# Rows of a graph attention kernel: TensorE turns replaced by a DRAM scratch and a broadcasting transfer

## Chip, cores, metric

One core of one Trainium2 chip. The metric is the device time of one execution in microseconds (us), lower is better.

## What is computed

Sixteen graphs of 1024 nodes with 256 features pass through four graph attention layers. Each layer is of this form (the four differ in the leaky function and in what follows):

```python
h  = relu(layernorm(x))
Wh = h @ W
f1, f2 = Wh @ a[:F], Wh @ a[F:]
e  = leaky_relu(f1[:, :, None] + f2[:, None, :])
e  = where(adj == 0, -1e9, e)
x  = x + softmax(e, -1) @ Wh          # layer 3: four heads of 64, then a normalisation
```

The exponential of a leaky sum is the larger (or smaller) of two products of exponentials. So the kernel needs no exponential for an edge: the weight of an edge is `max(r[i], c[j])`, times the mask, where r is a row vector and c a column. VectorE makes it with one instruction for 128 x 512 edges; such an instruction is called a weighing here. A turn is a transposition on TensorE: it takes a column of numbers, one in each of the 128 partitions, and lays it out as a row. SBUF is the memory that the engines work from, PSUM the one that TensorE writes to.

## The kernel before, where the change and the argument touch it

Two streams of batches (even and odd) are generators. Each `yield t` adds t to the stream's clock, and the stream that is behind goes on; this ranks their work. The built order interleaves them more finely than the text does. Each engine runs its own instructions in that order.

```python
    def weigh(column, c, mask, op, half, into):
        turned = psum.tile([P, HALF], F32, name="misc", bufs=3)
        for n in range(NG):                               # NG = 4 turns for a half row
            nc.tensor.transpose(
                turned[:, ts(n, P)], column(half * NG + n).to_broadcast([P, P]), ident)
        r = rows.tile([P, HALF], F32, name="row")
        nc.scalar.copy(r, turned)
        w = edges.tile([P, NI, HALF], F32, name="weights")
        into.append(w)
        for j in range(NI):                               # 8 weighings on VectorE
            nc.vector.scalar_tensor_tensor(
                w[:, j, :], r, c(j), mask[:, j, ts(half, HALF)], op0=op, op1=ALU.mult)
            if j % 4 == 3:
                yield 1.5

    # attend(), layers 0 to 2: first half's weights, then eight row blocks
            yield from weighing[0]
            for i in range(NI):
                t = next(weighing[1], None)
                ...
                for j in range(NI):
                    nc.tensor.matmul(acc, w[:, j, ts(i % NG, P)], V[:, j, : D + 1], ...)
                finish(i, acc)
                yield 3.6
                if i % 2 == 0 and i > 0:
                    project(then, xb, i // 2 - 1, following[1])   # the next layer's V, two blocks
                    yield 4.0

    # layer 3, for each of 4 heads x 2 halves
            for j in range(NI):
                nc.tensor.matmul(accT, V3[:, j, h, :], w[:, j, :], ...)
            sums = wide.tile([E + 1, HALF], F32, name="sums")
            nc.scalar.copy(sums, accT)
            next(coming, None)          # a step of the load of a later batch
            yield 7.5
            acc = psum.tile([P, NG, E + 1], F32, name="misc", bufs=3)
            for i in range(NG):
                nc.tensor.transpose(acc[:, i, :], sums[:, ts(i, P)], ident[: E + 1, : E + 1])
            ...
            yield 0.5

    streams = [[0.0, stream(0)], [LAG, stream(1)]]      # LAG = 120.0
```

Column `D + 2` of V (in layer 3, the last third of `ex`) gives a row.

## Time and profile before

| | before |
|---|---|
| time, median of 3 | 3343.65 us (3341.39 to 3344.26) |
| TensorE / VectorE / ScalarE busy | 93 / 75 / 29% |
| mean granted TensorE clock | 0.988 |

PE is TensorE and PEld its weight loads, DVE is VectorE, ACT ScalarE, POOL GpSimd, SP the engine that issues transfers. A busy share alone does not tell the bound; the prediction shows the lines that do.

### The profile page before, as it was taken

To read this page: it belongs to the slowest core of one execution; us is meant where nothing else is said; L and a number is where in the kernel's file an instruction comes from. 1 tells how busy PE (TensorE), PEld (TensorE's weight loads), DVE (VectorE), ACT (ScalarE), POOL (GpSimd) and SP (SyncE) were. 2 spreads that over 40 slices of the span, in tenths; PEclk is the share of its full clock that TensorE was granted. 3 is DMA by queue.
4 is the path that set the end of the run, shared out by engine and by line. 5 is a ranking of instruction groups with operands and counts; after the bars stand their busy time and mean duration, and the time that the engine had idled before them with its cause. 6 is when DMAs were issued, how large, how long until landed. Compare 5 with 4: busy or idle time off the path is not lost.

```text
span 3341.3 us, 38569 instructions
## 1 busy us (share of the span) xinstructions
PE 3103.0 (93%) x13702; PEld 2107.8 (63%) x13702; DVE 2504.0 (75%) x6140; ACT 974.3 (29%) x2081; POOL 1091.2 (33%) x1286
## 2 busy tenths in 40 slices
PE   6899999999989999899998999989999899998987
PEld 5765756657656675665756667566666666656652
DVE  5677787777778777787777877778777787777766
ACT  3423323232232322323233232332323223232121
POOL 1223324233242332424234142242323423234242
PEclk9999999999999999999999999999999999999998
DMA  4101101011010110101011010010101101000000
GB/s 115 26 4 16 32 11 40 7 17 29 13 39 8 16 29 13 38 10 16 26 16 35 10 42 4 13 35 13 39 4 17 32 13 38 7 10 13 1 13 14
DMA packets 55192, 73.19 MB, mean 22 GB/s; under 512 B 4049, under 2 KB 37969, under 8 KB 54993
## 3 DMA queue, kind: packets, MB, share of 16 engines
q0 software_dynamic: 18432, 33.56, 6.7%
q1 hardware_dynamic: 36560, 37.10, 3.5%
q8 instruction: 110, 1.80, 0.2%
q14 instruction: 90, 0.73, 0.1%
HBM read 87.43 MB, written 16.78 MB: 31 GB/s over the span
## 4 chain that ended last, share of the span: by engine, by line
DVE 45%; PE 42%; POOL 5%; ACT 4%; issue 3%; DMA 1%; SPq 0%; ACTq 0%; POOLq 0%; DVEq 0%
DVE weights L255 25%; PE acc L338 18%; PE acc L414 11%; PE projected L236 10%; DVE above L226 3%; PE misc L230 3%; DVE above L273 2%; DVE stats L220 2%; DVE above L274 2%; POOL x_b L275 2%; DVE V L290 2%; DVE y L380 1%; POOL y L379 1%; POOL rstd L212 1%; ACT below L271 1%
## 5 line engine op out<-in xcount | busy, mean ns | idle before, releaser
L338 PE MATMUL acc<-V,weights 128*128 128x257 f32 x6144 | 1454.9, 385 | 12.5 <-DVE weights L255 11.5
L338 PEld LDWEIGHTS acc<-V,weights 128*128 128x128 f32 x6144 | 1137.8, 191 | 208.9 <-DVE weights L255 47.2
L414 PE MATMUL acc<-weights,V 128*65 128x512 f32 x2048 | 914.2, 593 | 0.3 <-DVE weights L255 0.3
L255 DVE SCALAR_TENSOR_TENSOR weights<-row,ex,mask 128x512 f32<-128x512 f32 x1024 | 762.7, 784 | 2.7 <-ACT row L251 0.9
L255 DVE SCALAR_TENSOR_TENSOR weights<-row,V,mask 128x512 f32<-128x512 f32 x768 | 559.4, 776 | 53.0 <-ACT row L251 52.9
L414 PEld LDWEIGHTS acc<-weights,V 128*65 128x65 f32 x2048 | 278.7, 138 | 492.7 <-issue 474.0
L212 POOL TENSOR_TENSOR rstd<-rstd,minus_half 128x2 f32<-128x2 f32 (+1 forms) x320 | 311.3, 975 | 745.7 <-DVE rstd L211 703.2
L236 PE MATMUL projected<-W,hT 128*128 128x259 f32 (+1 forms) x2048 | 521.8, 398 | 14.8 <-ACT hT L232 11.3
L236 PEld LDWEIGHTS projected<-W,hT 128*128 128x128 f32 x2048 | 383.5, 195 | 130.1 <-ACT hT L232 60.4
L275 POOL TENSOR_TENSOR x_b<-x_b,above 128x256 f32<-128x256 f32 x256 | 227.5, 890 | 585.8 <-DVE above L274 532.5
L230 PE MATMUL misc<-ident,above 128*128 128x128 f32 x1024 | 189.1, 289 | 155.3 <-DVE above L226 108.6
L271 ACT ACTIVATE below<-acc,inv 128x256 f32<-128x256 f32 x256 | 120.0, 472 | 607.4 <-DVE inv L264 497.0
L232 ACT COPY hT<-misc 128x512 f32<-128x512 f32 x256 | 149.1, 586 | 495.8 <-PE misc L230 494.8
L230 PEld LDWEIGHTS misc<-ident,above 128*128 128x128 f32 x1024 | 113.7, 143 | 256.0 <-DVE above L226 120.3
L220 DVE BATCH_NORM_STATS2 stats<-x_b 128x6 f32<-128x256 f32 x512 | 206.7, 414 | 83.1 <-POOL x_b L275 78.9
L263 DVE TENSOR_SCALAR inv<-acc 128x1 f32<-128x1 f32 x256 | 37.3, 150 | 272.5 <-PE acc L338 272.3
L418 ACT COPY sums<-acc 65x512 f32<-65x512 f32 x128 | 74.0, 578 | 546.2 <-PE acc L414 546.1
L226 DVE TENSOR_SCALAR above<-x_b,mv 128x256 f32<-128x256 f32 x512 | 222.0, 443 | 3.8 <-POOL x_b L275 1.7
L105 POOL DMA_DIRECT2D adj_i<-in_adj_dram x128 | 77.1, 603 | 406.3 <-ACT sums L418 174.4
L290 DVE TENSOR_SCALAR V<-projected,rstd,V 128x256 f32<-128x256 f32 x256 | 134.8, 537 | 63.9 <-ACT V L286 62.9
L286 ACT ACTIVATE V<-projected,rstd 128x3 f32<-128x3 f32 x384 | 99.4, 261 | 262.0 <-PE projected L236 220.1
L314 POOL TENSOR_TENSOR x_b<-x_b,beta 128x256 f32<-128x256 f32 x128 | 117.3, 923 | 150.7 <-DVE above L226 148.6
(70 smaller groups left out, 2370.1 us busy)
## 6 DMA issues: line engine op xcount, KB each, us to landing
adj_i<-in_adj_dram POOLq DMA_DIRECT2D x128, 256.0 KB, 3.8
x_b<-in_x_dram SPq DMA_DIRECT2D x16, 1024.0 KB, 7.8
out_dram<-y SPq DMA_DIRECT2D x32, 512.0 KB, 3.8
W<-in_L_gnn_W_dram SPq DMA_DIRECT2D x3, 256.0 KB, 3.0
a_b<-in_L_gnn_a_dram SPq DMA_DIRECT2D x3, 256.0 KB, 6.4
a_b<-in_L_gnn_a_src_dram SPq DMA_DIRECT2D x1, 640.0 KB, 7.5
a_b<-in_L_gnn_a_dst_dram SPq DMA_DIRECT2D x1, 640.0 KB, 9.4
W<-in_L_gnn_W_dram SPq DMA_DIRECT2D x2, 128.0 KB, 8.9
```

The costliest lines, as they stand in the source:

```text
L212: nc.gpsimd.tensor_tensor(r, r, minus_half.to_broadcast([P, n]), op=ALU.pow)
L220: nc.vector.bn_stats(stats, xb[:, 2 * pair + n, :])
L226: nc.vector.tensor_scalar(above, xb[:, 2 * pair + n, :], mv[:, n, 0:1], 0.0, op0=ALU.subtract, op1=ALU.max)
L230: nc.tensor.transpose(turned[:, k, ts(n, P)], above[:, ts(k, P)], ident)
L232: nc.scalar.copy(hT, turned)
L236: nc.tensor.matmul(projected, hT[:, k, ts(n, P)], W[l][:, k, :], start=(k == 0), stop=(k == NK - 1),)
L255: nc.vector.scalar_tensor_tensor(w[:, j, :], r, c(j), mask[:, j, ts(half, HALF)], op0=op, op1=ALU.mult)
L271: nc.scalar.activation(below, acc[:, :D], AF.Exp, scale=inv)
L275: nc.gpsimd.tensor_add(xi, xi, above)
L290: nc.vector.tensor_scalar(V[:, i, :D], projected[:, :D], rstd, V[:, i, D : D + 1], op0=ALU.mult, op1=ALU.mult,)
L338: nc.tensor.matmul(acc, w[:, j, ts(i % NG, P)], V[:, j, : D + 1], start=(j == 0), stop=(j == NI - 1),)
L414: nc.tensor.matmul(accT, V3[:, j, h, :], w[:, j, :], start=(j == 0), stop=(j == NI - 1))
```

## The change

The intent: take 896 turns of 128x128 off the busiest engine and 224 row copies off ScalarE. The eight columns of a row are turned once, as a block of 8 x 128 (32 x 128 for layer 3's four heads), copied, written to DRAM in a line of 1024 numbers, and read back by one transfer that gives the line to all 128 partitions. To find room in SBUF, buffers are cut, and in layer 3 the four turns of the sums follow their matmuls at once.

```diff
+    def lay(b, columns, n):
+        turned = psum.tile([P, HALF], F32, name="misc", bufs=3)[: n * NI, :P]
+        nc.tensor.transpose(turned, columns, ident)
+        flat = wide.tile([P, P], F32, name="flat", bufs=1)[: n * NI]
+        nc.scalar.copy(flat, turned)
+        laid = dram.tile([n, N], F32, name=f"laid{b % 2}_{n}")
+        nc.sync.dma_start(laid.rearrange("n (i p) -> (n i) p", p=P), flat)
+        return laid
+
+    def spread(b, laid):
+        r = rows.tile([P, N], F32, name=f"row{b % 2}")
+        nc.sync.dma_start(r, on_all_partitions(laid, N))
+        return r
 # attend()
+            r = spread(b, lay(b, V[:, :, D + 2], 1)[0])
+            yield 0.5
 # layer 3
+        laid = lay(b, ex[:, 2 * H :, :].rearrange("p h i -> p (h i)"), H)
+        spreads = [spread(b, laid[h]) for h in range(2)]
         def weigh3(n):
+                if half == 0 and 0 < h < H - 1:
+                    spreads.append(spread(b, laid[h + 1]))
-            sums = wide.tile([E + 1, HALF], F32, name="sums")
+            sums = wide.tile([P, HALF], F32, name="wide")[: E + 1]
             nc.scalar.copy(sums, accT)
-            next(coming, None)
-            yield 7.5
             ...                                # turns of the sums, division
-            yield 0.5
+            next(coming, None)
+            yield 8.0
 # cut: the turns in weigh; rows bufs 4 -> 2 (of twice the size), below bufs 3 -> 2, ones moved,
 # ex stored heads first
```

More of the change, by code (lines that the diff above doesn't have):

```diff
@@ L85, in short_path @@
     nc.vector.memset(minus_half, -0.5)
-    ones = const.tile([P, P], F32, name="ones")
-    nc.vector.memset(ones, 1.0)
     squares = const.tile([P, B, NI], F32, name="squares")
@@ L146, in short_path @@
     with tc.tile_pool(name="prep", bufs=2) as prep:
+        ones = prep.tile([P, P], F32, name="ones")
+        nc.vector.memset(ones, 1.0)
         for l in range(3):
@@ L200, in short_path @@
     edges = ctx.enter_context(tc.tile_pool(name="edges", bufs=4))
-    rows = ctx.enter_context(tc.tile_pool(name="rows", bufs=4))
+    rows = ctx.enter_context(tc.tile_pool(name="rows", bufs=2))
+    dram = ctx.enter_context(tc.tile_pool(name="dram", bufs=2, space=bass.MemoryType.DRAM))
     single = ctx.enter_context(tc.tile_pool(name="single", bufs=1))
@@ L240, in project, with lay, spread, weigh @@
             evict(2 * pair + n, projected, rstd[:, n : n + 1])
-    def weigh(column, c, mask: bass.AP, op, half: int, into: list):
-        turned = psum.tile([P, HALF], F32, name="misc", bufs=3)
-        for n in range(NG):
-            nc.tensor.transpose(
-                turned[:, ts(n, P)], column(half * NG + n).to_broadcast([P, P]), ident
-            )
-        r = rows.tile([P, HALF], F32, name="row")
-        nc.scalar.copy(r, turned)
+    def lay(b: int, columns: bass.AP, n: int) -> bass.AP:
+        turned = psum.tile([P, HALF], F32, name="misc", bufs=3)[: n * NI, :P]
[5 more added lines that the diff above has]
+        return laid
+    def spread(b: int, laid: bass.AP) -> bass.AP:
+        r = rows.tile([P, N], F32, name=f"row{b % 2}")
+        nc.sync.dma_start(r, on_all_partitions(laid, N))
+        return r
+    def weigh(r: bass.AP, c, mask: bass.AP, op, half: int, into: list):
         w = edges.tile([P, NI, HALF], F32, name="weights")
@@ L255, in weigh @@
             nc.vector.scalar_tensor_tensor(
-                w[:, j, :], r, c(j), mask[:, j, ts(half, HALF)], op0=op, op1=ALU.mult
+                w[:, j, :], r[:, ts(half, HALF)], c(j), mask[:, j, ts(half, HALF)], op0=op, op1=ALU.mult
             )
@@ L269, in add_elu @@
         inverse(inv, acc[:, D : D + 1])
-        below = work.tile([P, D], F32, name="below")
+        below = work.tile([P, D], F32, name="below", bufs=2)
         nc.scalar.activation(below, acc[:, :D], AF.Exp, scale=inv)
@@ L302, in begin3 @@
             V3 = nodes.tile([P, NI, H, E + 1], F32, name="V")
-            ex = last["ex"] = small.tile([P, NI, 3 * H], F32, name="ex", bufs=2)
+            ex = last["ex"] = small.tile([P, 3 * H, NI], F32, name="ex", bufs=2)
             def evict3(i: int, projected: bass.AP, rstd: bass.AP):
-                nc.scalar.activation(ex[:, i, :], projected[:, D:], AF.Exp, scale=rstd)
+                nc.scalar.activation(ex[:, :, i], projected[:, D:], AF.Exp, scale=rstd)
                 nc.scalar.mul(h3[:, i, :], projected[:, :D], rstd)
-                q = ex[:, i, :H].unsqueeze(2)
+                q = ex[:, :H, i : i + 1]
                 nc.gpsimd.tensor_mul(
@@ L321, in attend @@
             halves = []
+            r = spread(b, lay(b, V[:, :, D + 2], 1)[0])
+            yield 0.5
             weighing = [
-                weigh(
-                    lambda i: V[:, i, D + 2 : D + 3], lambda j: V[:, j, D + 1 : D + 2],
-                    mask, op, half, halves,
-                )
+                weigh(r, lambda j: V[:, j, D + 1 : D + 2], mask, op, half, halves)
                 for half in range(NH)
@@ L400, in weigh3 @@
             if h < H:
+                if half == 0 and 0 < h < H - 1:
+                    spreads.append(spread(b, laid[h + 1]))
                 yield from weigh(
-                    lambda i: ex[:, i, 2 * H + h : 2 * H + h + 1],
-                    lambda j: ex[:, j, H + h : H + h + 1], mask, ALU.max, half, halves,
+                    spreads[h], lambda j: ex[:, H + h, j : j + 1], mask, ALU.max, half, halves
                 )
```

## The prediction

> **What bounds the kernel now.** I read first the page's busy table, to see which engine has least room.
>
> ```profile
> span 3341.3 us, 38569 instructions
> PE 3103.0 (93%) x13702; PEld 2107.8 (63%) x13702; DVE 2504.0 (75%) x6140; ACT 974.3 (29%) x2081; POOL 1091.2 (33%) x1286
> ```
>
> TensorE (PE) is busy 93% of the span, VectorE (DVE) 75%, ScalarE (ACT) 29%. Next the chain that ended last, since a share of busy time does not say who makes whom wait:
>
> ```profile
> DVE 45%; PE 42%; POOL 5%; ACT 4%; issue 3%; DMA 1%; SPq 0%; ACTq 0%; POOLq 0%; DVEq 0%
> ```
>
> The end is reached through TensorE and VectorE by turns. So TensorE time taken out is worth nearly its full size only where TensorE is the one that is behind; elsewhere VectorE's weights (25% of the chain, line 255) decide. Third, the groups by line, for the instructions that the change removes:
>
> ```profile
> L247 PE MATMUL misc<-ident,ex 128*128 128x128 f32 x512 | 77.6, 272 | 0.0
> L247 PE MATMUL misc<-ident,V 128*128 128x128 f32 x384 | 63.6, 276 | 2.3 <-ACT mask L122 1.8 <-ACT V L286 0.3
> L251 ACT COPY row<-misc 128x512 f32<-128x512 f32 x224 | 129.5, 587 | 89.4 <-PE misc L247 88.6
> L255 DVE SCALAR_TENSOR_TENSOR weights<-row,V,mask 128x512 f32<-128x512 f32 x768 | 559.4, 776 | 53.0 <-ACT row L251 52.9
> ```
>
> 896 turns (512 in layer 3, 384 in layers 0 to 2) are busy 141.2 us, but busy time of pipelined matmuls contains their tails. What a turn costs TensorE is the distance between starts, and the chain in order of time, between 1636 and 1665 us, shows that where TensorE is the one that is behind:
>
> ```profile
> 1642.80 0.66 PE misc L247 x6
> 1643.46 3.47 PE acc L338 x16
> 1646.93 6.87 PE acc L414 x16
> ```
>
> Six turns in 0.66 us: 0.11 us each, against 0.27 us in the group's mean. Likewise 0.217 us for a layer 0-2 attention matmul and 0.429 us for a layer 3 one. Last I looked at the stretches of the span. Two stages alternate: stretches with a layer 3 in one of the two batch streams, and stretches with attention of layers 0 to 2 in both.
>
> ```profile
> 960.00:1020.00 60.00, 51.28 (x242) 39.95 (x241) 45.18 (x125) 17.85 (x42) 32.18 (x43) 0.97 0.17 44
> 1020.00:1160.00 140.00, 135.78 (x596) 86.82 (x595) 104.99 (x251) 42.25 (x86) 39.27 (x42) 1.00 0.09 14
> ```
>
> The columns after the length are busy time of TensorE, its weight loads, VectorE, ScalarE and GpSimd. TensorE is 97% busy in the second kind (a layer 3), only 85% in the first, where two streams wait on their own chains (normalise, turn, project, weigh).
>
> **What the Trainium skill says.** (1) "Perfetto Trace Analysis", Identifying the Most-Contended Engine: matmul busy time is no good measure, since pipelined instructions look different from what they cost. The trace agrees: 0.27 us busy against a pitch of 0.11 us for these turns. (2) "TensorE: Matmul & The Clock Gate", Part 4: a 128x128 turn measured about 275 ns in a kernel. The trace agrees (272 and 276 ns), but that is latency and not occupancy. (3) "DMA: Bandwidth & Descriptors", Anatomy of one DMA: about 2.0 us fixed plus bytes over 436 GB/s (measured there for the software path). For 512 KB that gives 3.2 us; the page's DMA issues show 3.8 us for as much, by the hardware path:
>
> ```profile
> out_dram<-y SPq DMA_DIRECT2D x32, 512.0 KB, 3.8
> a_b<-in_L_gnn_a_dram SPq DMA_DIRECT2D x3, 256.0 KB, 6.4
> ```
>
> The second line is a broadcasting load at the start, where many loads overlap. (4) The same page, Rules for kernel authors: a DMA that reads what an earlier DMA wrote must wait for the earlier one's completion. So the new way pays two landings one after the other. No run yet shows that pair.
>
> **The change, part by part.** *Removed:* 896 turns x 0.11 us = 98.6 us of TensorE. 224 row copies on ScalarE, 129.5 us. *Added:* per batch three small turns for layers 0 to 2 and one for layer 3, 64 in all; their moving side is still the 128-wide identity, so 64 x 0.11 = 7 us on TensorE. 64 copies of at most 32x128 on ScalarE, at some 0.27 us (as the 128x3 activation of line 286 takes) 17 us. Net on TensorE -92 us, 2.7% of the span; ScalarE -112 us, off the chain but for the turns of the projections that it frees sooner. VectorE does the same 1792 weighings of 0.66 us pitch. *Transfers:* 64 writes of 4 or 16 KB and 112 broadcasts (7 rows x 16 batches) of 128 x 4 KB = 512 KB. At 3.8 us landing, 112 x 3.8 = 426 us in which something is under way, spread over the span with DMA now a tenth busy or less in its middle: bandwidth is not the question, latency is.
>
> *Moved.* In the kernel before, a row of one half needs four of the eight columns, and those are ready before the last pair of node blocks is projected. The timeline of ScalarE at one start shows it:
>
> ```profile
> 1672.68 0.59 ACT L251 COPY row<-misc 128x512 f32<-128x512 f32 x1
> 1674.09 0.26 ACT L286 ACTIVATE V<-projected,rstd 128x3 f32<-128x3 f32 x1 [0.81 <-PE projected L236]
> 1674.90 0.26 ACT L286 ACTIVATE V<-projected,rstd 128x3 f32<-128x3 f32 x1 [0.55 <-PE projected L236]
> ```
>
> and VectorE there:
>
> ```profile
> 1673.61 0.74 DVE L255 SCALAR_TENSOR_TENSOR weights<-row,V,mask 128x512 f32<-128x512 f32 x1
> 1674.38 0.55 DVE L290 TENSOR_SCALAR V<-projected,rstd,V 128x256 f32<-128x256 f32 x1
> ```
>
> The first weighing (1673.6) starts 1.5 us before the last column exists (1675.16). Going through the 48 starts of layers 0 to 2 by the turns of V in the timeline, the first weighing begins between 3 us before the last column and 4 us after it, mostly 1 to 2 us before. Afterwards the whole row needs all eight columns, and then: turn 0.3 + copy 0.3 + write 2.0 (the skill's fixed part) + broadcast 3.8 = 6.4 us, or some 5.5 us if an unloaded 512 KB broadcast takes 3 us. Call it 6 us. The last weighing of that half moves less, since its last columns were late before too: I take 5 us of delay for a stream at each start. Four starts a batch (three layers and layer 3's first head; heads 1 to 3 are fetched a head ahead) make 20 us a batch, 16 batches in two streams: 160 us along each stream.
>
> How much of that reaches the end? While one stream waits, TensorE can work for the other, and one attention half or layer 3 half there is 3.5 to 7 us of it. In the 140 of some 200 us of a period with a layer 3 the delay should be mostly covered; with both streams in layers 0 to 2, where TensorE is already 15% idle, mostly not. I choose a third: 160/3 = 53 us. Of the 92 us saved I choose 95% for the 512 turns of layer 3 (56 us gross) and 80% for the other 384 (42 us gross), less the 7 added: 53 + 34 - 7 = 80 us. The buffers cut (rows, below, sums in the shared wide ring) and the output turns moved up behind their matmuls cost some waits, the ScalarE time freed gives some back: I put them at 10 us lost. Sum: 3343 - 80 + 53 + 10 = 3326 us; I shade it to 3310, since the change's retuned steps look like those of someone who had seen a gain.
>
> **Rivals.** *Full gain.* The wait is covered everywhere by the other stream: 3343 - 85 = 3258 us, 2.5% faster. For it: 97% TensorE in the layer 3 stretches, and ScalarE freed. Against it: VectorE's 45% of the chain and the start rows that VectorE already waits for, 53.8 us in 26 waits. *The new wait wins.* Rows arrive 6 us late at 64 starts, VectorE stands in order behind them, and half or more of 320 us shared by two streams comes through: 160 - 80 gives 3420 us. For it: half-rows are used before the last column now, and both streams together leave 15% of TensorE idle in the common stretches. Against it: several weighings and matmuls of the other stream are nearly always ready. *VectorE takes over.* TensorE's time falls, VectorE's does not, and the weights bind the layer 3 stretches: then half the 53 us there is lost, and the time is about 3335 us. For it: VectorE is 105 of 140 us busy there, in bursts near 100%. Against it: the mean still leaves 25%. *The transfer is slow.* A broadcast reads the same 4 KB 128 times; if it takes 6.4 us as the loads at the start did, each start loses another 2.5 us: some 25 us more at the end.
>
> **Range and chances.** The full gain is 3258, the ordinary case 3310 to 3335, the bad case 3420. 8 in 10: 3225 to 3400. Over 2% faster is under 3277 and needs nearly the full gain: 0.33. Over 2% slower is above 3411: 0.13. Within 2%: 0.54. Predicted: 3310 us.
>
> **What would show it.** Right if TensorE's busy time falls by 110 to 150 us (busy, with tails) while the span falls by less; ScalarE by about 110 us; if VectorE's weighings name the DMA of a row as what ended their wait, some 1 to 4 us each at up to 64 starts; if write and broadcast together land 5 to 7 us after the copy. Wrong if the weighings hardly wait for rows (full gain), if the landing is over 9 us, or if layer 3's rows of heads 1 to 3 are waited for too, which I take to be fetched in time.

## The result

The changed kernel takes 3665.64 us (median of 4, 3661.47 to 3669.08) against 3343.41 us: the ratio is 1.0964, with a 95% interval of 1.0945 to 1.0983. Here and below a ratio is the mean time of one kernel's fast runs over that of the other's of the same rounds, so not quite the ratio of the medians. I had said 3310, with 3400 as the upper end.

The page of the changed kernel, busy table and the chain by engine:

```profile
span 3659.8 us, 37115 instructions
PE 3155.2 (86%) x12870; PEld 2077.5 (57%) x12870; DVE 2561.0 (70%) x6140; ACT 884.8 (24%) x1921; POOL 1080.4 (30%) x1286
...
PE 45%; DVE 37%; POOL 6%; DMA 5%; ACT 4%; issue 3%; SPq 0%; ACTq 0%; POOLq 0%; DVEq 0%
```

Every engine's share is lower than before: all wait more. DMA stands in the chain with 5% instead of 1%. TensorE has 832 instructions less and is busy 52 us longer. The groups by line, changed kernel, tell that the work itself went as planned:

```profile
L346 PE MATMUL acc<-V,weights 128*128 128x257 f32 x6144 | 1519.6, 396 | 172.7 <-DVE weights L264 172.7
...
L264 DVE SCALAR_TENSOR_TENSOR weights<-row,V,mask 128x512 f32<-128x512 f32 x768 | 589.4, 822 | 33.4 <-DMA row<-laid 33.2
...
L246 PE MATMUL misc<-ident,V 128*8 128x128 f32 x48 | 13.1, 274 | 3.5 <-ACT V L295 3.5
```

The turns are gone but for 64 small ones (48 of them in the last line). What is new is the idle time before the attention matmuls: 172.7 us against 12.5. Line 346 here is line 338 of the kernel before, whose group is:

```profile
L338 PE MATMUL acc<-V,weights 128*128 128x257 f32 x6144 | 1454.9, 385 | 12.5 <-DVE weights L255 11.5
```

The view of who waited for whom, kernel before:

```profile
DVE weights L255 <- ACT row L251: 53.8, 26, 4.7
PEld acc L338 <- DVE weights L255: 47.2, 114, 1.5
PE acc L338 <- DVE weights L255: 11.5, 15, 1.2
```

and changed (total us, number of waits, longest):

```profile
PEld acc L346 <- DVE weights L264: 217.7, 129, 9.5
PE acc L346 <- DVE weights L264: 172.7, 71, 9.2
DVE weights L264 <- DMA row<-laid: 63.6, 28, 13.7
```

TensorE now waits up to 9 us for weights; 1.5 us was the longest. VectorE itself names the row's transfer in 28 waits only, all of them at the starts, ending 5 to 8 us after the turn; mostly it still had other work when the row came. One start shows how that fits together. First the transfers of the changed kernel, timeline of SP:

```profile
1391.28 0.29 SPq L250 DMA_DIRECT2D laid<-flat  x1
1392.49 0.32 SPq L256 DMA_DIRECT2D row<-laid  x1
```

the timeline of TensorE in the same stretch:

```profile
1388.32 2.02 PE L237 MATMUL projected<-W,hT 128*128 128x259 f32 x8 [1.17 <-ACT hT L233]
1390.69 0.28 PE L246 MATMUL misc<-ident,V 128*8 128x128 f32 x1 [0.35 <-ACT V L295]
1397.95 1.23 PE L346 MATMUL acc<-V,weights 128*128 128x257 f32 x2 [6.99 <-DVE weights L264]
```

and of VectorE:

```profile
1395.32 0.69 DVE L400 TENSOR_TENSOR y<-y,rstd 128x512 f32<-128x512 f32 x1 [1.78 <-POOL rstd L213]
1396.04 6.18 DVE L264 SCALAR_TENSOR_TENSOR weights<-row,V,mask 128x512 f32<-128x512 f32 x6
```

The write is asked for at 1391.28, the broadcast 1.21 us later, when the write has landed, and the first weighing starts 3.55 us after that. TensorE does one turn and then nothing for 7 us: the other stream is finishing layer 3 on VectorE (line 400) and gives no matmul in this stretch. Then the weighings bring one block each 0.66 us or more (the first three lie 1.7 to 1.8 us apart), and TensorE follows at their pace. This start is one of the worse ones. In 17 of the 48 starts of layers 0 to 2, and in 8 of the 16 of layer 3, TensorE stands still for more than 3.4 us in one go; in the others it is less.

The pitch of a kind of instruction is the usual time from its start to the next instruction's start. Over the 64 starts I counted, for each kernel, how much longer TensorE's instructions lay apart than their pitch in the 14 us from just before the last column is turned: some 56 us before, 407 us after. The difference, 351 us, is more than the whole loss of 322. The same count over the whole span gives 352 us before and 759 after: 407 us more lost, less 89 us of work saved, is the 318 us by which the profiled span grew.

A second effect follows. The table of stretches, changed kernel (length, busy time of PE, PEld, DVE, ACT, POOL, granted clock, DMA share, GB/s):

```profile
1390.00:1404.00 14.00, 6.21 (x15) 4.07 (x14) 11.81 (x17) 1.15 (x3) 4.53 (x3) 0.66 0.16 46
1404.00:1440.00 36.00, 35.98 (x144) 21.54 (x143) 30.66 (x69) 9.61 (x18) 7.85 (x8) 0.99 0.15 30
```

The clock granted is 0.66 in the mean of these 14 us, wait included. In the records it halves 3.6 us after TensorE fell idle and stays halved for 10.2 us, that is into the matmuls that follow. The Trainium skill, "TensorE: Matmul & The Clock Gate", HAM oscillation, warns of it: idle gaps of more than about 3.4 us bring the clock back to half. This start agrees, but the rule does not cover what the traces show. Leaving out the first 30 and the last 20 us, the clock halves 17 times in the kernel before, and the longest idle gap in the 6.8 us before any of these is 3.1 us (in one it is only 1.4); in the changed kernel 41 of 71 halvings follow gaps under 3.4 us. What all of them share is a TensorE that was busy for at most 55% of the 3.4 us before. So several short gaps can do what one long gap does.

The mean clock gives the time at half clock, 2 x (1 - clock) x span: 80 us before (0.988), 461 us after (0.937). What that costs can be estimated from the same traces. At half clock matmuls that follow each other directly start at about twice their pitch; added up, the excess is 28 us before and 122 us after. So some 94 of the 407 us more lost are the clock's, and the rest, some 313 us, is waiting.

### The profile page after: what moved, and what is told of

It reads as the page before. It is cut to its first block, busy times and chain, and to the rows that moved or that the text cites. A ratio compares the mean times of both kernels' runs of the same rounds, so it can differ in the third digit from the quotient of the medians.

```text
span 3659.8 us, 37115 instructions
## 1 busy us (share of the span) xinstructions
PE 3155.2 (86%) x12870; PEld 2077.5 (57%) x12870; DVE 2561.0 (70%) x6140; ACT 884.8 (24%) x1921; POOL 1080.4 (30%) x1286
## 4 chain that ended last, share of the span: by engine, by line
PE 45%; DVE 37%; POOL 6%; DMA 5%; ACT 4%; issue 3%; SPq 0%; ACTq 0%; POOLq 0%; DVEq 0%
DVE weights L264 21%; PE acc L346 17%; PE acc L426 14%; PE projected L237 10%; DMA row<-laid 3%; DVE above L227 3%; DVE above L282 2%; PE misc L231 2%; DVE stats L221 2%; POOL y L387 2%; DVE above L283 1%; POOL x_b L284 1%; ACT below L280 1%; POOL rstd L213 1%; DMA laid<-flat 1%
## 5 line engine op out<-in xcount | busy, mean ns | idle before, releaser
L346 PE MATMUL acc<-V,weights 128*128 128x257 f32 x6144 | 1519.6, 396 | 172.7 <-DVE weights L264 172.7
L346 PEld LDWEIGHTS acc<-V,weights 128*128 128x128 f32 x6144 | 1182.2, 198 | 426.5 <-DVE weights L264 217.7
L426 PE MATMUL acc<-weights,V 128*65 128x512 f32 x2048 | 954.5, 610 | 68.7 <-DVE weights L264 39.4
L264 DVE SCALAR_TENSOR_TENSOR weights<-row,V,mask 128x512 f32<-128x512 f32 x768 | 589.4, 822 | 33.4 <-DMA row<-laid 33.2
L237 PE MATMUL projected<-W,hT 128*128 128x259 f32 (+1 forms) x2048 | 552.6, 415 | 17.2 <-ACT hT L233 16.1
L237 PEld LDWEIGHTS projected<-W,hT 128*128 128x128 f32 x2048 | 399.8, 203 | 152.1 <-ACT hT L233 76.3
L227 DVE TENSOR_SCALAR above<-x_b,mv 128x256 f32<-128x256 f32 x512 | 209.5, 420 | 8.7 <-POOL x_b L284 4.9
L430 ACT COPY wide<-acc 65x512 f32<-65x512 f32 x128 | 74.3, 580 | 572.3 <-PE acc L426 572.3
L272 DVE TENSOR_SCALAR inv<-misc 128x4 f32<-128x4 f32 x128 | 19.7, 154 | 256.4 <-PE misc L433 256.2
L282 DVE TENSOR_SCALAR above<-acc,inv 128x256 f32<-128x256 f32 x256 | 123.5, 483 | 64.7 <-ACT below L280 63.4
```

Source lines behind the costliest of these rows:

```text
L227: nc.vector.tensor_scalar(above, xb[:, 2 * pair + n, :], mv[:, n, 0:1], 0.0, op0=ALU.subtract, op1=ALU.max)
L237: nc.tensor.matmul(projected, hT[:, k, ts(n, P)], W[l][:, k, :], start=(k == 0), stop=(k == NK - 1),)
L264: nc.vector.scalar_tensor_tensor(w[:, j, :], r[:, ts(half, HALF)], c(j), mask[:, j, ts(half, HALF)], op0=op, op1=ALU.mult)
L282: nc.vector.tensor_scalar(above, acc[:, :D], inv, 0.0, op0=ALU.mult, op1=ALU.max)
L426: nc.tensor.matmul(accT, V3[:, j, h, :], w[:, j, :], start=(j == 0), stop=(j == NI - 1))
```

## The experiments

The starts are the 48 places where an attention of layers 0 to 2 begins and the 16 where layer 3 does. There a row cannot be fetched ahead; the rows of heads 1 to 3 can. The theories are those of the expectations. The changed kernel, with which most are compared, took 3666 us.

### The parts alone, and the row without its dependence

**out_only**: before, with the new output step alone.

```diff
             nc.scalar.copy(sums, accT)
-            next(coming, None)
-            yield 7.5
 # cut: turns and division
-            yield 0.5
+            next(coming, None)
+            yield 8.0
```

> The kernel before with one part of the change alone: the four output turns of a layer 3 half follow their matmuls at once, the load step and the 8.0 step come after them; rows by TensorE turns as before, sums in a ring of its own. Theory A (the late rows are the loss): within 2% of before, 3300 to 3400 us. Theory B (the output step is the loss, since TensorE and VectorE stand for the copy of the sums): 3500 us or more, and the turns of the sums wait for ScalarE by some 100 us in all.

Measured: 3437 us, ratio 1.0272. Neither range: worse than theory A, not enough for B.

**rows_only**: the changed kernel with the old output step.

```diff
             nc.scalar.copy(sums, accT)
+            next(coming, None)
+            yield 7.5
 # cut
-            next(coming, None)
-            yield 8.0
+            yield 0.5
```

> The changed kernel with the output step put back as it was before (load step and 7.5 between the copy of the sums and their turns, 0.5 after); the sums stay in the shared wide ring, since a ring of their own does not fit. Theory A (late rows): 3580 us or more, nearly all of the loss stays. Theory B (output step): 3300 to 3400 us.

Measured: 3673 us, 1.0978. The whole loss is there without the new step. Theory B falls.

**ones_row**: changed; every broadcast reads a line of ones. Its output is wrong, which doesn't matter for the time.

```diff
-        nc.sync.dma_start(r, on_all_partitions(laid, N))
+        nc.sync.dma_start(r, on_all_partitions(even[0], N))   # even: written once at the start
```

> The changed kernel, wrong on purpose: every broadcast reads a DRAM row of ones that was written once at the start, so that no row depends on columns and each can land early; turns, copies, writes to DRAM, 112 broadcasts of 512 KB and the output step all stay. Theory A (waiting for late rows): at or under the kernel before, 3230 to 3340 us, and the TensorE clock back at 0.98 or more. Theory B (output step, buffers or DMA traffic): still over 3550 us.

Measured: 3296 us, 0.9854, so 370 us less than the changed kernel. All turns, copies and transfers are still made. The loss is thus in the dependence of the row on its columns, with the order of instructions that goes with it, and not in the traffic or the buffers. (The built order is not quite the same: in 78% of the places in TensorE's order the instruction is of the same kind as in the changed kernel.) The waits of this kernel, where line 349 is the attention matmul:

```profile
PEld acc L349 <- DVE weights L267: 12.1, 14, 1.4
PE acc L349 <- DVE weights L267: 3.4, 7, 0.5
```

The waits of up to 9 us are gone. The clock is 0.973, better than 0.937 but not the 0.98 that I expected.

**heads**: changed, but with turns at the 64 starts, half by half as before; only heads 1 to 3 go by DRAM.

```diff
-            r = spread(b, lay(b, V[:, :, D + 2], 1)[0])
-            yield 0.5
+            turned = turn(b, lambda i: V[:, i, D + 2 : D + 3])      # four turns a half, as before
-        spreads = [spread(b, laid[h]) for h in range(2)]
+        spreads = [turn(b, lambda i: ex[:, 2 * H, i : i + 1]), spread(b, laid[1])]
 # cut: the helper turn, which makes a half row as before; weigh asks for it
```

> The changed kernel with its transfers only where they can be fetched ahead: rows of heads 1 to 3 of layer 3 by DRAM, the rows of layers 0 to 2 and of head 0 by TensorE turns of each half as before; the new output step and the cut buffers stay. Theory A (late rows at the 64 starts): 384 turns or 42 us of TensorE less than before and no late row, 3290 to 3360 us. Theory B (output step or buffers): 3500 us or more.

Measured: 3313 us, 0.9907 (0.989 to 0.992), correct. It is faster than both kernels, the changed one by 353 us. VectorE never waits for a row's transfer here (no wait over 0.15 us). It has 512 turns (56 us at 0.11 us) that the changed one has not, so a start by DRAM costs (353 + 56) / 64 = 6.4 us on average.

### Landing or late columns

**by_half**: changed, with the starts' rows laid and spread in two halves, so that the first needs four columns only.

```diff
-            r = spread(b, lay(b, V[:, :, D + 2], 1)[0])
+            r = spread_halves(b, lambda half: V[:, ts(half, NG), D + 2])   # also head 0
```

> The changed kernel with the rows of the 64 starts laid and broadcast half by half, so that the first half needs only four columns, which are ready before the last projections; still two transfers one after the other for each. Theory A1 (the two landings, 5.2 us, are the loss): still 3550 us or more. Theory A2 (the row waiting for all eight columns is the loss): 3300 to 3420 us. Half and half: 3450 to 3550 us.

Measured: 3550 us, 1.0617: at the edge of theory A1; 115 us of the loss go.

**late_turns**: heads; in layers 0 to 2 the first half's row takes the last four columns. Its output is wrong, which doesn't matter for the time.

```diff
-            turned = turn(b, lambda i: V[:, i, D + 2 : D + 3])
+            turned = turn(b, lambda i: V[:, (i + NG) % NI, D + 2 : D + 3])
```

> The heads kernel, wrong on purpose: in layers 0 to 2 the first half's row is turned by TensorE from columns 4 to 7 and the second half's from 0 to 3, so that no weighing can start before the last column, without any transfer there. Theory A1 (landings): within 1.5% of heads, 3300 to 3360 us. Theory A2 (late columns): 3420 us or more.

Measured: 3351 us, 1.0026; 38 us more than heads, within A1's range. Late columns by themselves are the smaller part, by this run and by by_half, the landings the larger one.

**heads_all**: heads with head 0 by DRAM too.

```diff
-        spreads = [turn(b, lambda i: ex[:, 2 * H, i : i + 1]), spread(b, laid[1])]
+        spreads = [spread(b, laid[h]) for h in range(2)]
```

> The heads kernel with head 0 of layer 3 by DRAM too, so that 16 of the 64 starts wait for two landings and the 48 of layers 0 to 2 do not. In the changed kernel's trace TensorE loses 55 us in the 14 us after the last column of those 16 starts and 352 us at the 48. Theory A says 3313 + 50, less 14 us for the 128 turns gone: 3340 to 3370 us. If layer 3 itself were the trouble: over 3450 us.

Measured: 3398 us, 1.0163. 86 us more than heads for 16 starts, over 5 us each; I expected half of that. The same count as above gives 101 us of lost TensorE time at these 16 starts, against 7 in heads.

**second_halves**: heads, with the second half of each start's row by DRAM.

```diff
         def of(half):
+            if half == 1:
+                # cut: one turn of four columns, copy, write, broadcast of 512 numbers
             # cut: the four turns, as before
```

> The heads kernel with the second half's row of each of the 64 starts laid and broadcast through DRAM as well, the first half's by turns: the second half is first needed some 5 us of weighings and several row blocks later, so its landings should be covered. Theory A: 256 turns or 28 us less of TensorE, 3280 to 3315 us, the fastest so far. If any landing in the path of a start costs, over 3350 us.

Measured: 3354 us, 1.0038, 41 us more than heads. My expectation failed. The landing is mostly not what is waited for: VectorE waits for these rows' transfers 11 times, 14.2 us in all and 1.9 us at most. Which wait it is instead stays open, and 41 us are within what a shift of the streams does (see before_lag).

**twice**: changed, with a copy from DRAM to DRAM between write and broadcast.

```diff
-        nc.sync.dma_start(laid.rearrange("n (i p) -> (n i) p", p=P), flat)
+        nc.sync.dma_start(first.rearrange("n (i p) -> (n i) p", p=P), flat)
+        nc.sync.dma_start(laid..., first...)
```

> The changed kernel with a third transfer in series at each lay: the columns are written to a first DRAM row, copied there to a second one, and that is broadcast. Nothing else differs. Theory A (each start waits its landings out in full): the added landing, some 1.5 to 2.5 us, shows at 48 to 64 starts nearly whole, 80 to 160 us more than the changed kernel, 3750 to 3830 us. Rival C (the loss comes from another order of instructions, and the other stream covers a longer wait as it covered some of this one): under 3710 us.

Measured: 3762 us, 1.1242; 97 us more. In the traces the median time from the copy to the landed row rises from 5.17 to 7.17 us, 2.0 us at 64 starts, 128 us: three quarters of it reach the end. TensorE's order is nearly the changed kernel's (the same kind of instruction in 95% of the places), so this run tells most plainly that the landing itself is paid for.

### Clock and order

**warm**: changed, with eight idle matmuls after each lay of layers 0 to 2.

```diff
             r = spread(b, lay(b, V[:, :, D + 2], 1)[0])
+            for k in range(8):
+                nc.tensor.matmul(warm, ident, W[0][:, k % NK, :], start=(k == 0), stop=(k == 7))
```

> The changed kernel with eight matmuls of 128x259 on constants (16 instructions, 3.5 us) after each of the 48 lays of layers 0 to 2, to a PSUM tile that nobody reads, so that TensorE has something to do while a row lands and its clock is not halved. If the halved clock after the waits is a large part of the loss (about 95 us of small excess lies in halved stretches), the time falls, 3560 to 3640 us, with the halved clock's share down. If the clock matters little, or the matmuls stand in the way of others, 3670 us or more (168 us would be the cost if nothing of them were hidden).

Measured: 3591 us, 1.0730. More work on the busiest engine made the kernel 74 us faster, with the mean clock at 0.962 (273 us at half clock by the formula above, against 461). That agrees with the halved clock being a part of the loss, but does not show it by itself: the order of the rest changed with it, and 74 us are no more than a shift of the streams moves the changed kernel (after_lag below).

**late_yield**: changed, with 7.0 for 0.5 after the row is asked for in layers 0 to 2.

```diff
             r = spread(b, lay(b, V[:, :, D + 2], 1)[0])
-            yield 0.5
+            yield 7.0
```

> The changed kernel with 7.0 in place of 0.5 after the row is asked for, so that some 6.5 us more of the other stream's work ranks ahead of this stream's weighings. If the wait is exposed since the order of instructions leaves nothing of the other stream to do (theory A with a cause in the order), 3500 to 3620 us. If the other stream has nothing to give at those places, within 1.5% of the changed kernel, 3610 to 3720 us.

Measured: 3395 us, 1.0149. One number gives 271 us back, while the median from copy to landed row stays at 5.2 us. The timeline of TensorE at one start of this kernel:

```profile
1295.35 0.27 PE L246 MATMUL misc<-ident,V 128*8 128x128 f32 x1
1295.46 3.60 PE L426 MATMUL acc<-weights,V 128*65 128x512 f32 x8
1298.92 0.46 PE L433 MATMUL misc<-ident,wide 65*128 65x65 f32 x4
1299.22 0.61 PE L119 MATMUL misc<-ident_b,adj_i 128*128 128x128 bf16 x8
1299.67 3.60 PE L426 MATMUL acc<-weights,V 128*65 128x512 f32 x8
```

Here the other stream's layer 3 matmuls stand behind the turn, and TensorE never stops. That is so at part of the starts: in 21 of the 48 of layers 0 to 2 TensorE stands still for less than 1 us in one go, and in none of the changed kernel's. So a landing costs where the order leaves nothing of the other stream to do, and costs little or nothing where it does.

**heads_old_step**: heads with the old output step (diff as in rows_only).

> The heads kernel with the output step of the kernel before (load step and 7.5 between the copy of the sums and their turns). The new step alone cost 2.7% in the kernel before, and nothing in the changed one. If it costs by itself, 3230 to 3290 us, the fastest; if it only mattered together with the old rows, 3300 to 3330 us as heads.

Measured: 3344 us, 0.9995. The new step is worth 32 us here, and cost 93 us in out_only. It has no sign of its own.

**yield_7_7** and **yield_12_12**: late_yield with a step after layer 3's rows are asked for too, of 7.0, and with 12.0 in both places.

```diff
         spreads = [spread(b, laid[h]) for h in range(2)]
+        yield 7.0
```

> late_yield with 7.0 after the two rows of layer 3 are asked for as well, where there was no step. Order theory: the 75 to 80 us that TensorE loses at those 16 starts shrink by half or more, 3310 to 3360 us. If the landing is exposed at layer 3 whatever the order: 3380 to 3410 us as late_yield.

> The same with 12.0 in both places, more than landing and first weighing take. Order theory with room left: 3270 to 3330 us, near the row of ones (3296). If the other stream has no more ready work than 7.0 ranked ahead, or the streams starve each other: 3350 us or more.

Measured: 3481 us (1.0415) and 3556 us (1.0636). Both expectations failed. In yield_7_7 the 16 layer 3 starts lose 11 us where they lost 82 in late_yield, but the 48 others lose 224 against 159.

**heads_all_yield**: heads_all with 7.0 there (diff as above).

> heads_all with 7.0 after the rows of layer 3 are asked for. heads_all lost 85 us against heads by waiting at 16 starts. Order theory: most of it comes back and the 128 further turns saved show, 3300 to 3340 us. If the landing is exposed there whatever the order: 3380 to 3410 us.

Measured: 3415 us, 1.0209; no gain against heads_all. The starts do gain, 101 us become 13. It is given back elsewhere, in good part in the projections, as the waits show. heads_all:

```profile
PEld misc L231 <- DVE above L227: 170.2, 196, 3.8
PE misc L231 <- DVE above L227: 140.3, 159, 3.3
```

heads_all_yield:

```profile
PEld misc L231 <- DVE above L227: 215.7, 240, 4.4
PE misc L231 <- DVE above L227: 193.1, 186, 3.5
```

TensorE waits 53 us more (its loads 46) for the normalised input of the next layer. A wait that the order hides at one place can come up at another.

**no_transfer**: heads with all rows by turns.

```diff
-        spreads = [turn(...), spread(b, laid[1])]
+        spreads = [of_head(0), of_head(1)]      # of_head: turns, half by half
-                    spreads.append(spread(b, laid[h + 1]))
+                    spreads.append(of_head(h + 1))
```

> The heads kernel with all rows by TensorE turns, each half when its columns are there: the new output step, the cut buffers and the shared ring of the change without any transfer. If the rest of the change costs nothing by itself: heads plus the 384 turns it saves, 3313 + 42, 3335 to 3365 us. If the output step costs 2.7% as it did alone: 3400 us or more.

Measured: 3401 us, 1.0174: 58 us more than before and 88 more than heads, between the two expectations. This kernel has every turn of the kernel before, with the cut buffers and the new step: together these cost 58 us here, about what a shift of the streams does.

**before_lag** and **after_lag**: the two kernels with another lag between the streams.

```diff
-    LAG = 120.0
+    LAG = 108.0      # after_lag: 112.0
```

> The kernel before with a lag of 108 in place of 120 between the two streams and nothing else. If the order of the work matters little where no landing waits: within 1%, 3310 to 3375 us. If a mere shift moves the time by 2% or more (up to 3450 us), differences of 1 to 3% between the variants tell nothing of a mechanism.

> The changed kernel with a lag of 112 in place of 120, which gives the streams about the share of a batch's period between them that late_yield gives (120 of some 283 against 112 of some 264). If late_yield gained by where the streams meet: 3400 to 3550 us. If it gained by the work ranked ahead at the starts themselves: 3620 to 3700 us.

Measured: before_lag 3398 us, 1.0166; after_lag 3577 us, 1.0701, 89 us less than the changed kernel and between its two expectations: part of late_yield's 271 us may thus come from where the streams meet. A shift that alters no instruction moves the time by 56 to 89 us. So the kernels within 3% of before (out_only, no_transfer, late_turns, second_halves, heads_all, heads_all_yield, heads_old_step, and the gain of heads over before) do not prove a mechanism by their times alone, and neither does warm's 74 us; by_half's 115 us are little more. The differences of 270 us and more (ones_row, heads and late_yield against the changed kernel) are three times that or more.

## Why the prediction was wrong

- **The work saved** was right: 896 turns gone and 64 added, 92 us forecast; counted at its usual pitch, TensorE's work fell by 89 us. The sign that I named for it was wrong: TensorE's busy time rose by 52 us. Busy time holds matmuls that run at half clock (attention matmuls have a mean of 396 ns against 385), so it does not measure work where the clock changes. ScalarE fell by 89.5 us, of 112 predicted.
- **The landing** was right: 5 to 7 us forecast, an estimate that took the write from the skill's figure; 5.2 us is the median from the start of the copy to the landed row over the 64 starts (4.9 us from the copy's end). The write took 1.2 us of it, not the 2.0 of the skill's fixed part; the broadcast 3.6 us.
- **The step that failed** is "How much of that reaches the end? [...] I choose a third: 160/3 = 53 us". What is shown: where the term puts 53 us, TensorE lost 351 us more at the 64 starts than before. With no dependence on the columns 370 us come back, and with turns at the starts 353. Two errors lie in that term. I divided 64 delays by two streams, as if the two streams' waits always ran side by side. But both streams wait on the one TensorE, and their waits add: 64 delays of 5 us are 320 us, and some 313 us of waiting is what TensorE lost more. And I took the other stream's work to be there in most stretches. In the built order often too little was behind the turn: at 25 of the 64 starts TensorE stands still for more than 3.4 us in one go, as at 1390.69.
- **What I left out** is the clock: 461 us at half clock against 80 in the traces, some 94 us of the loss by the estimate above. warm agrees, but its 74 us do not measure the clock alone.
- **The signs of being wrong** that I named did not come: the landing was under 9 us, and rows of heads 1 to 3 were not waited for. They looked at VectorE's waits for rows (63.6 us in all); the loss stood in TensorE's waits for the weights.
- **Late columns**, which I put first in "Moved", are the smaller part: late_turns cost 38 us, inside what a shift of the streams does, and by_half gave back 115 of 322 us.
- **The rivals.** "The new wait wins" (3420) was the right one, and too small. "VectorE takes over" and "The transfer is slow" are out: VectorE's part of the chain fell from 45 to 37%, and the broadcast took 3.6 us. That the retuned steps pointed to a gain was no evidence and should not have moved the number.
- **Heads 1 to 3** fetched ahead were right: all waits for rows lie at the starts, and heads, which has these transfers alone, waits for no row.

Open: how much of the loss is the landing as such and how much the order. late_yield shows that most of it is not forced. But more of the same step lost it again, and no order tried brought the full change under the kernel before. Whether heads gains its 0.9% by the turns saved or by its order is open too, since a lag alone moves the kernel before by 1.7%.

## What to carry to other kernels

A transfer in place of engine work can be free where it is asked for a stage ahead (heads 1 to 3; that it gains is not shown beyond what a shift of the streams does), and is a loss where the next work of the stream hangs on it and nothing else is in line: ask not how busy the engines are on average, but which instruction stands next in the bound engine's order while the transfer lands. Waits can also halve TensorE's clock for what follows (80 us at half clock before, 461 after), so they cost more than themselves. In a kernel of interleaved streams, shift the streams against each other once as a control, before a difference of 1 to 3% is explained.

## What the Trainium skill lacked or had wrong

- "DMA: Bandwidth & Descriptors", Anatomy of one DMA, gives about 2.0 us fixed for a transfer by the software path. Here, by the hardware path, a 4 KB write (16 KB at layer 3) from SBUF to DRAM issued from SP let its dependent transfer issue 1.23 us later (median of 64), a 512 KB broadcast from DRAM landed 3.64 us after issue (median of 112), and the copy of 4 or 16 KB from DRAM to DRAM added 2.0 us to the chain. No figure stands there for such a chain of two, 5.2 us here with the copy before it.
- "Perfetto Trace Analysis", Identifying the Most-Contended Engine, says that matmul busy time is no good measure since pipelined instructions look smaller in the trace. Here they look larger: a turn is shown with 0.27 us where the next starts after 0.11 us.
- "TensorE: Matmul & The Clock Gate", HAM oscillation, puts its rule as idle gaps of 3.4 us. In the kernel before all 17 halvings follow gaps of 3.1 us or less, in the changed one 41 of 71 follow gaps under 3.4 us; see the result.
